# Cross attention in a decoder layer: one load of queries for the row maxima of two heads, on keys whose masked places are filled

## The chip, the cores and the metric

One core of a Trainium2 chip runs the whole kernel in one launch. The metric is the device time in microseconds, from a median of runs. Its engines work side by side, each on its own queue in program order: TensorE (PE: products, and PEld: the loads of its stationary operand), VectorE (DVE), ScalarE (ACT), GpSimd (POOL) and SyncE (SP), which here only issues DMAs. Products land in PSUM, which this kernel uses as eight banks of 128 x 512 fp32.

## The reference

Four sequences of 1024 rows and 256 features pass a decoder layer: windowed causal self-attention, cross attention on 77 context rows, and a quantised feed-forward part. The change touches the middle one alone (16 heads of 16 features):

```python
x = x + attn(layernorm(x), w_qkv, w_out)                      # windows of 128, causal
x = x + xattn(layernorm(x), ctx, ctx, mask, Wq, bq, Wk, bk, Wv, bv, Wo, bo)
x = x + ffn(layernorm(x), ...)                                # int8-like rounding

def xattn(Q, K, V, mask, Wq, bq, Wk, bk, Wv, bv, Wo, bo):
    q = heads(Q @ Wq.T + bq)          # [4, 16, 1024, 16]
    k = heads(K @ Wk.T + bk)          # [4, 16, 77, 16]
    v = heads(V @ Wv.T + bv)
    scores = einsum('bhqd,bhkd->bhqk', q, k) / 4
    scores = where(mask == 0, -inf, scores)
    attn = softmax(scores)            # needs the row maximum first
    return merge(einsum('bhqk,bhkd->bhqd', attn, v)) @ Wo.T + bo
```

In the inputs all rows of the mask are alike (the same keys are masked for every query).

## The kernel before

**Heads and groups.** The 16 heads stand in two groups g of eight. In a group, partitions are cut into four strips j of 32; a strip holds two heads, `o` = 0 and 1, of 16 features each. A projected tile `q[g, o]` (128 partitions x 1024 queries) keeps the rows of head o in each strip; the other head's 16 rows are zero and partly used as extra rows: one will hold minus the row maximum, one is constant 1. For keys `kx` the matching rows hold 1 and the mask bias (0 or -1e30). So one product of depth 32 gives score + mask - maximum, and ACT only takes the exponential.

**Two products of the same scores.** For each (g, o) the scores are formed twice. `maxima` forms them with queries on partitions (bank `sc_n`, line 742 for cross attention: stationary a tile of 128 queries, moving 77 keys); DVE reduces them to the row maxima (line 768). `put_maxima` turns the maxima on TensorE (line 779), copies them to SBUF on ACT (`mxT`, line 783) and writes them with four DMAs on SP's queue (line 786) into a row of each strip of `q[g, o]`. Then `weights` forms the scores with keys on partitions (bank `sc_t`, line 841: stationary 77 keys, moving 512 queries), ACT takes exp (line 844), and `weighted_values` multiplies with the values (line 866).

**Units and slots.** The work is a list of units (job, g, o, u). Jobs are S0 S1 S2 X0 S3 X1 X2 X3 (S self-attention, X cross attention, the digit is the sequence); an S job has 16 units, an X job 8 (u = two halves of 512 queries). A loop over slots issues, in this order: `early` work, values of an older unit (`ps_av`, line 856 or 866, with DVE's lines 880 to 902), tasks (projections `ps_p`, out-projections `ps_op`, turns `ps_t`, preparation), DVE work beside, `puts`, then `maxima` of the unit five slots ahead (LEAD = 5), then `weights` of the slot's own unit. Each engine takes what is issued in that order. PSUM banks go round all these uses, so a product can wait for ACT or DVE to have read a bank.

**Projections.** `project` forms 512 queries of all heads of a group (16 instructions of line 304), and ACT writes two masked copies, one for each o (line 363 for cross attention: bias and scale both from per-partition columns).

**When maxima are put.** For (g, o) whose first unit has slot tau, with m units per (g, o), `put_maxima` is in slot tau + m - LEAD: tau - 1 for S jobs (m = 4), tau - 3 for X jobs (m = 2).

**Preparation of cross attention** is a list of pieces, three slots apart from slot 5 on, one step a slot: biases; Wk; the context (loaded by one DMA, turned by eight products of line 490, copied by DVE, line 495); keys (line 502, written by four DVE instructions of line 510); Wv; values of the context; the mask row; Wq; Wo. All of it falls into jobs S0 and S1. A branch on whether the mask's rows are alike picks one of two whole programs; with these inputs the first, `alike`, runs.

## Time and profile before

| | us |
|---|---|
| median of 3 runs (lowest, highest) | 669.54 (668.43, 670.75) |
| the profiled execution: its time | 669.67 |
| its span, first to last instruction | 668.0 |
| mean granted TensorE clock | 0.981 |
| line 742 (maxima of X), 1024 instructions from 270.8 to 524.1: product busy, load busy | 36.5, 31.7 |
| line 768 (DVE maxima of X), 128 x 468 ns | 51.9 |
| line 363 (ACT, projected queries of X), 32 x 774 ns | 23.1 |
| line 779 (turn of maxima), 32 instructions | 9.1 |
| line 786 (DMAs of maxima), 128 of 4 KB, issue of one on SP's queue | 0.63 |
| keys and context, lines 490, 502 (PE), 495, 510 (DVE), once | 0.8, 2.3, 0.9, 2.1 |

An fp32 product is two instructions in the trace (two loads, two products), so the 16 products of a unit of line 742 stand as 32. Durations of products are modelled and overlap; what a group of them takes is read from the start of the first to the start of what follows. By stages: X0's maxima run from 270 to 307 us beside S2 and X0's own weights, X1's from 399 to 435, X2's and X3's to 524; the feed-forward part starts near 560.

### The profile page before, as it was taken

Reading aid. Unit: us, or ns where it says so; the run is one execution under the profiler, and the core shown is the slowest. Engines: PE = TensorE matmul, PEld = TensorE weight load, DVE = VectorE, ACT = ScalarE, POOL = GpSimd, SP = SyncE. Lnnn points to the kernel's source line nnn. Section 1 sums busy time; section 2 is a strip of 40 time slices with the busy share of each in tenths; the row PEclk is TensorE's granted clock in tenths of the full one; section 3 lists DMA queues with packets and bytes.
Section 4 is the critical chain, followed back from the end, with each engine's and each line's share of the span. In section 5 each row is a group of like instructions: output and inputs, shape, how many; then the busy total and the mean of one; then the engine's idle time right before and its main releaser. Section 6 shows DMA issues by size and latency. Waiting matters only on the chain.

```text
span 668.0 us, 20224 instructions
## 1 busy us (share of the span) xinstructions
PE 619.9 (93%) x7862; PEld 355.8 (53%) x7862; DVE 542.9 (81%) x1922; ACT 367.8 (55%) x672; POOL 268.9 (40%) x520
## 2 busy tenths in 40 slices
PE   9989999999999998999999999999999997888774
PEld 6466556566555565654446666554443445333564
DVE  6588887878769799768997996897978787799896
ACT  2535454653555644655565356447556465688392
POOL 3135632455324567660035777616611141111032
PEclk9979799999999999999999999999999999899898
DMA  8100100000000000000000000000000020000057
GB/s 290 46 2 17 38 2 3 20 5 4 19 26 11 11 2 19 5 19 12 9 11 11 11 24 26 5 3 4 3 3 4 4 95 17 1 0 1 1 96 163
DMA packets 18081, 17.43 MB, mean 26 GB/s; under 512 B 2999, under 2 KB 17336, under 8 KB 17976
## 3 DMA queue, kind: packets, MB, share of 16 engines
q1 hardware_dynamic: 15239, 13.69, 6.4%
q0 software_dynamic: 1904, 1.84, 2.1%
q8 instruction: 64, 1.05, 0.7%
q10 hardware_dynamic: 832, 0.53, 0.3%
q14 instruction: 42, 0.34, 0.2%
HBM read 9.47 MB, written 6.03 MB: 23 GB/s over the span
## 4 chain that ended last, share of the span: by engine, by line
PE 62%; DVE 25%; ACT 6%; issue 5%; POOL 1%; DMA 0%; DVEq 0%; ACTq 0%
PE ps_p L304 13%; PE ps_av L856 8%; PE sc_t L812 8%; PE sc_n L727 7%; PE ps_op L304 6%; PE ps_av L866 4%; PE sc_t L841 3%; PE ps_v L304 3%; PE sc_n L742 3%; DVE junk L757 3%; DVE bnst L192 2%; DVE o_sb L880 2%; PE ps_idle L117 2%; PE pg L1393 2%; DVE aT L902 2%
## 5 line engine op out<-in xcount | busy, mean ns | idle before, releaser
L757 DVE CUSTOM_DVE_ANT_0 junk<-sc_n,cboth 128x256 bf16<-128x256 f32 (+1 forms) x512 | 172.5, 402 | 34.5 <-PE sc_n L727 34.4
L822 ACT ACTIVATE pt<-sc_t 128x512 f32<-128x512 f32 (+1 forms) x256 | 125.4, 576 | 92.6 <-PE sc_t L812 92.6
L826 POOL TENSOR_SCALAR_AFFINE_SELECT pt<-pt 128x256 f32<-128x256 f32 x256 | 102.0, 407 | 114.8 <-ACT pt L822 104.6
L812 PE MATMUL sc_t<-shared 32*128 32x256 f32 (+1 forms) x1024 | 91.1, 382 | 2.4 <-DVE mx L757 0.6
L844 ACT ACTIVATE ptx<-sc_t 77x512 f32<-77x512 f32 x128 | 65.3, 597 | 36.9 <-PE sc_t L841 36.9
L727 PE MATMUL sc_n<-shared 32*128 32x256 f32 (+1 forms) x1024 | 79.1, 398 | 1.3 <-ACT shared L369 0.7
L812 PEld LDWEIGHTS sc_t<-shared 32*128 32x128 f32 x1024 | 68.0, 188 | 15.6 <-ACT shared L363 2.5
L320 POOL TENSOR_SCALAR xn<-x,mv,rs 128x256 f32<-128x256 f32 x56 | 70.0, 1256 | 0.0
L160 POOL TENSOR_SCALAR ve<-mv 128x4 f32<-128x4 f32 x20 | 4.6, 232 | 156.4 <-DVE mv L194 156.3
L880 DVE STREAM_TRANSPOSE o_sb<-ps_av 128x512 f32<-128x512 f32 x63 | 45.0, 714 | 26.0 <-PE ps_av L856 15.9
L727 PEld LDWEIGHTS sc_n<-shared 32*128 32x128 f32 x1024 | 49.8, 190 | 30.2 <-DVE mx L757 11.1
L856 PE MATMUL ps_av<-pt,vt 128*32 128x256 f32 (+1 forms) x1152 | 60.1, 352 | 3.0 <-DVE mx L757 2.6
L304 PE MATMUL ps_p<-shared,w_s 128*32 128x512 f32 x512 | 60.5, 595 | 2.4 <-DVE mx L768 1.3
L768 DVE TENSOR_REDUCE mx<-sc_n 128x4 f32<-128x308 f32 x128 | 51.9, 468 | 8.5 <-PE sc_n L742 8.3
L856 PEld LDWEIGHTS ps_av<-pt,vt 128*32 128x32 f32 x1152 | 35.2, 111 | 31.7 <-DVE mx L757 6.4
L841 PE MATMUL sc_t<-shared,kx 32*77 32x512 f32 x256 | 45.9, 599 | 0.0
L757 DVE DVE_READ_ACCUMULATOR2_ANT mx<- 128x1 f32 x512 | 42.5, 83 | 0.1
L866 PE MATMUL ps_av<-ptx,vx 77*32 77x512 f32 x256 | 36.0, 605 | 3.4 <-DVE mx L768 2.5
L363 ACT ACTIVATE shared<-ps_p,bq_p,qrows 128x512 f32<-128x512 f32 x32 | 23.1, 774 | 26.0 <-PE ps_p L304 26.0
L742 PEld LDWEIGHTS sc_n<-kx,shared 32*128 32x128 f32 x1024 | 31.7, 186 | 10.1 <-DVE mv L194 1.7
L742 PE MATMUL sc_n<-kx,shared 32*128 32x77 f32 x1024 | 36.5, 277 | 0.0
L1408 ACT ACTIVATE act<-pg,gsc 128x512 f32<-128x512 f32 x44 | 29.2, 688 | 11.6 <-PE pg L1393 9.0
(201 smaller groups left out, 986.7 us busy)
## 6 DMA issues: line engine op xcount, KB each, us to landing
x<-in_x_dram SPq DMA_DIRECT2D x8, 512.0 KB
shared<-mxT SPq DMA_DIRECT2D x128, 4.0 KB
out_dram<-x SPq DMA_DIRECT2D x7, 256.0 KB
out_dram<-shared POOLq DMA_DIRECT2D x7, 256.0 KB, 4.5
out_dram<-shared SPq DMA_DIRECT2D x7, 256.0 KB
w_s<-in_L_attn_w_qkv_dram SPq DMA_DIRECT2D x2, 384.0 KB
raw_d<-in_L_ffn_w_down_dram SPq DMA_DIRECT2D x2, 352.0 KB
raw_f<-in_L_ffn_w_gate_dram SPq DMA_DIRECT2D x5, 128.0 KB
```

Source lines behind the costliest of these rows:

```text
L304: nc.tensor.matmul(out[r], lhsT[:, r], rhs, skip_group_check=True, **on)
L320: eng.tensor_scalar(xn, xb[job.b][:, t, :], job.st[hf].mv[:, i, 0:1], job.st[hf].rs[:, i : i + 1], ALU.subtract, ALU.mult,)
L727: nc.tensor.matmul(banks[j][:, (i + 1) * 2 * P - n : (i + 1) * 2 * P], q[r, t * P : (t + 1) * P], k[r, k0 * P : k0 * P + n], start=True, s ...
L742: nc.tensor.matmul(banks[j][:, i * SK : (i + 1) * SK], q[r, t * P : (t + 1) * P], k[r, :], start=alike, stop=alike or i == HT - 1,)
L757: nc.vector.tensor_tensor_reduce(out=junk[:, 2 * P - n :], in0=banks[j][:, (i + 1) * 2 * P - n : (i + 1) * 2 * P], in1=cboth[:, 2 * P - n ...
L812: nc.tensor.matmul(banks[j][:, w : w + n], k[r, t * P : (t + 1) * P], q[r, t * P : t * P + n], start=True, stop=True,)
L822: nc.scalar.activation(pt.rearrange("p i a q -> p (i a q)")[:, :w], banks[j][:, :w], AF.Exp)
L826: nc.gpsimd.affine_select(out=pt[:, :, 0, :], in_=pt[:, :, 0, :], compare_op=ALU.is_ge, fill=0.0, base=0, pattern=[[0, 2], [1, P]], channe ...
L841: nc.tensor.matmul(banks[j][:SK], k[r, :], q[r, s], start=alike, stop=True)
L844: nc.scalar.activation(pt, banks[j][:SK], AF.Exp)
L856: nc.tensor.matmul(ps[j * SL : (j + 1) * SL, (a0 - t0) * P : (a1 - t0) * P], slot_of(job.vs[kb // 2][:, kb % 2], heads[j]), job.pts[g, o, ...
L866: nc.tensor.matmul(ps[j * SL : (j + 1) * SL, :], slot_of(vx[:, job.b], heads[j]), job.pts[g, o, j, hf], start=True, stop=True,)
```

## The change

Only the program for alike rows is changed, and in it cross attention alone.

1. **Preparation.** Before the context is loaded, a new piece `for_maxima` is put into the list, with four steps: `load_keymask` (the context, now by two DMAs, and one mask row on 77 partitions), `pick` (a 77 x 77 matrix that takes every unmasked key to itself and every masked key to the first unmasked one: seven DVE instructions and one POOL select), `context(True)` (the context times that matrix), and `keys_for_maxima` (keys from it without mask rows, written to a new tile `kmx` in which both heads' keys of a strip stand side by side, zero in the other head's rows). The plain context is loaded and turned again three slots later; all later pieces come three slots later.
2. **Projection.** For o = 0 ACT writes both heads' queries unmasked (scale an immediate, bias `bq_s`); o = 1 as before.
3. **Maxima.** One product of a tile of 128 queries with 154 columns of `kmx` gives the scores of both heads. A unit now takes two query tiles of both heads in place of four tiles of one: 8 products of 154 columns in place of 16 of 77, and DVE reduces the same 308 columns a bank.
4. **Masking later.** `part_heads` rewrites `q[g, 0]` in place on ACT (128 x 1024) to what it was before: head 0's rows and the constant row.
5. **Put.** One `put_maxima` a group in place of two: one turn and one copy of 64 rows, then eight DMAs. It and `part_heads` are in slot tau + 2m - LEAD = tau - 1 of o = 0.

```diff
@@ project
-                if job.kind == "X":
+                if job.kind == "X" and job.both and o == 0:
+                    nc.scalar.activation(
+                        dst, ps, AF.Identity, bias=job.bqs[:, g : g + 1], scale=QSCALE
+                    )
+                elif job.kind == "X":
@@ prep_cross: biases
+                    nc.vector.tensor_scalar(bq_s, raws["q"], QSCALE, None, ALU.mult)
...
+                            if alike and name == "k":
+                                nc.vector.tensor_copy(raws["bk"][:, :, o], dst[:, :, o])
@@ prep_cross: context
                 def load_context():
-                    raws["c"] = stage.tile([SK, B, D], F32, name="craw", tag="stage")
-                    nc.sync.dma_start(out=raws["c"], in_=ctx_in.rearrange("b k d -> k b d"))
+                    for h in range(2):
+                        raws["c", h] = stage.tile([SK, B // 2, D], F32, name="craw", tag="stage")
+                        nc.sync.dma_start(
...
-                def context():
+                def context(chosen=None):
...
+                            if chosen is None:
+                                nc.tensor.transpose(
+                                    ps[:, b * SK : (b + 1) * SK], raw, ident[:SK, :SK]
+                                )
+                            else:
+                                nc.tensor.matmul(
+                                    ps[:, b * SK : (b + 1) * SK],
+                                    raw,
+                                    raws["pick"],
+                                    start=True,
+                                    stop=True,
+                                )
...
+                def load_keymask():
+                    load_context()
+                    raws["v"] = small.tile([SK, SK], I32, name="vrow", bufs=1)
+                    nc.sync.dma_start(out=raws["v"], in_=mask[0, :].partition_broadcast(SK))
+                def pick():
+                    nc.vector.tensor_scalar(valid, raws["v"], 0.0, None, ALU.not_equal)
+                    nc.gpsimd.affine_select(
+                        out=below,
...
+                    nc.vector.tensor_reduce(held_by[:, 0:1], below, AX.X, ALU.max)
+                    nc.vector.tensor_tensor(sel, valid, ident[:SK, :SK], ALU.mult)
+                    nc.vector.tensor_reduce(held_by[:, 1:2], sel, AX.X, ALU.max)
+                    nc.vector.tensor_tensor(
+                        first, held_by[:, 1:2], held_by[:, 0:1], ALU.is_gt
+                    )
+                    nc.vector.tensor_scalar(valid, valid, -1.0, 1.0, ALU.mult, ALU.add)
+                    nc.vector.scalar_tensor_tensor(sel, valid, first, sel, ALU.mult, ALU.add)
+                def keys_for_maxima():
+                    for g in range(NP):
...
+                        for o in range(NS):
+                            nc.vector.tensor_scalar(
+                                kmx[:, g, :, o * SK : (o + 1) * SK],
+                                ps[:, : B * SK].rearrange("p (b k) -> p b k", k=SK),
+                                rows[o],
+                                raws["bk"][:, g, o : o + 1],
...
+                for_maxima = [load_keymask, pick, lambda: context(True), keys_for_maxima]
                 return [
                     [load_biases, biases],
                     transposed(Wk, "wk_x"),
+                    *([for_maxima] if alike else []),
                     [load_context, context],
@@ maxima
+                if job.kind == "X" and alike:
+                    pair = NH * o + u
+                    w = NS * SK
+                    for i in range(2):
+                        t = 2 * pair + i
+                        for j in range(NJ):
+                            r = slice(j * SL, (j + 1) * SL)
+                            nc.tensor.matmul(
+                                job.nb[j][:, i * w : (i + 1) * w],
+                                job.q[g, 0][r, t * P : (t + 1) * P],
+                                kmx[r, g, job.b, :],
+                                start=True,
+                                stop=True,
+                            )
+                    for j in range(NJ):
+                        nc.vector.tensor_reduce(
+                            job.mx[g][:, :, j, 2 * pair : 2 * pair + 2].rearrange("p o i -> p i o"),
+                            job.nb[j][:, : 2 * w].rearrange("p (i o k) -> p i o k", i=2, o=NS),
...
@@ put_maxima
+            def part_heads(job, g, o):
+                q = job.q[g, 0]
+                nc.scalar.activation(q, q, AF.Identity, bias=nextrow[o], scale=rows[o])
...
+                nc.tensor.transpose(ps[:n, :P], mx, ident)
+                nc.scalar.copy(mxT[:n], ps[:n, :P])
+                for k in range(n // NT):
+                    o_, j = divmod(k, NJ) if two else (o, k)
+                    row = j * SL + (1 - o_) * HD
                     nc.sync.dma_start(
-                        out=job.q[g, o][row : row + 1, :],
-                        in_=mxT[j * NT : (j + 1) * NT, :],
+                        out=job.q[g, o_][row : row + 1, :],
+                        in_=mxT[k * NT : (k + 1) * NT, :],
                     )
@@ the list of slots
-                        puts.setdefault(tau + m - LEAD, []).append((job, g, o))
+                        if S_ or not alike:
+                            puts.setdefault(tau + m - LEAD, []).append((job, g, o))
+                        elif o == 0:
+                            at = tau + NS * m - LEAD
+                            early.setdefault(at, []).append((part_heads, (job, g, o)))
+                            puts.setdefault(at, []).append((job, g, o))
```

## The prediction

> **What bounds the kernel now.** I read the busy shares first, then the chain of waits over cross attention, then the timeline of single slots there, because a share over the span hides which wait ends last.
>
> ```profile
> PE 619.9 (93%) x7862; PEld 355.8 (53%) x7862; DVE 542.9 (81%) x1922; ACT 367.8 (55%) x672; POOL 268.9 (40%) x520
> ```
>
> TensorE looks full. In the chain of waits (start, length, what) a typical slot of X2 reads so:
>
> ```profile
> 456.06 1.00 PE ps_av L866 x8
> 457.05 1.72 PE ps_p L304 x16
> 458.77 1.06 PE sc_n L742 x32
> 459.83 1.69 PE sc_t L841 x8
> 461.52 1.04 PE ps_av L866 x8
> ```
>
> All five are TensorE's, the maxima of line 742 among them; but line 841 took 1.69 there. A slot in which it waits for nothing, and then one like that above (timeline; start, length, engine, line):
>
> ```profile
> 509.18 1.04 PE L841 MATMUL sc_t<-shared,kx 32*77 32x512 f32 x8
> 510.14 1.06 PE L866 MATMUL ps_av<-ptx,vx 77*32 77x512 f32 x8
> ...
> 468.66 1.13 PE L742 MATMUL sc_n<-kx,shared 32*128 32x77 f32 x32
> 468.80 1.45 ACT L363 ACTIVATE shared<-ps_p,bq_p,qrows 128x512 f32<-128x512 f32 x2 [1.10 <-PE ps_p L304]
> 469.61 1.76 PE L841 MATMUL sc_t<-shared,kx 32*77 32x512 f32 x8
> 470.30 0.21 PEld L841 LDWEIGHTS sc_t<-shared,kx 32*77 32x77 f32 x2 [0.53 <-ACT shared L363]
> 471.31 1.07 PE L866 MATMUL ps_av<-ptx,vx 77*32 77x512 f32 x8
> ```
>
> Free, line 841 needs 0.96 us to the next product. In the second slot it needs 1.70: its last bank is the projection's, and ACT's two copies of line 363 release that at 470.25. They start at 468.80, when the projection has ended, whatever line 742 does meanwhile. So there the slot's length is projection, then 1.45 of ACT, then two products of 0.49 on one strip; line 742 lies beside ACT.
>
> I sorted all 32 units of line 742 by what ends the line 812 or 841 behind them. 14 wait for ACT's projection copies as here (at 270.8, 274.9, 285.0, 294.4, 398.9, 403.1, 409.6, 442.1, 453.4, 458.7, 468.7, 487.5, 498.9, 504.3). Two wait for ACT's copy of line 341 (306.6, 413.3). 14 lie in stretches where the chain runs through DVE (lines 880 to 902, 192, then 768) and TensorE waits at its end. Two are free: 300.7 and 508.2, and behind the second DVE follows with 0.12 us of slack.
>
> **The change: the maxima.** A unit of line 742 takes 0.95 us from 403.07 to 404.02, 29.7 ns an instruction. The price of 154 columns is not in the trace; the nearest rows are self-attention's:
>
> ```profile
> 311.61 0.94 PE L727 MATMUL sc_n<-shared 32*128 32x128 f32 x16
> 312.37 1.04 PE L841 MATMUL sc_t<-shared,kx 32*77 32x512 f32 x8
> ...
> 317.77 1.15 PE L727 MATMUL sc_n<-shared 32*128 32x256 f32 x16
> 318.74 1.62 PE L841 MATMUL sc_t<-shared,kx 32*77 32x512 f32 x8
> ```
>
> 16 of 256 columns take 0.97 us (60.6 ns each); 8 of 128 and 8 of 256 take 0.76, so 128 columns cost 34.4. By interpolation 154 cost 39.7, the unit 16 x 39.7 = 0.63, a saving of 0.32; at the price of 256 columns it is nothing. Over 32 units that is 10.1 us of TensorE, but on the path only where TensorE ends last: the two free units (0.32 and 0.12), almost nothing elsewhere: 0.5 us. DVE's reductions are the same 128 of 468 ns.
>
> The Trainium skill (Perfetto Trace Analysis, "Identifying the Most-Contended Engine") holds matmul busy time for no measure of how full TensorE is, and load busy time for a better one: 93% against 53% here. By the 93% this part would save some 9 us; by the rule TensorE has room and it saves next to nothing, which the waits above bear out.
>
> **Fewer turns.** 8 of the 16 X instructions of line 779 go, 0.21 us each (453.21 to 453.42). Four stand in stretches of DVE and cost nothing there. At 409.4, 453.2 and 498.7 ACT's copy after line 363 is what goes (about 0.13 us later than the projection's own release), at 300.5 the whole 0.21: 0.6 us, of which I count 0.4. DVE is late next.
>
> **Cheaper projection copies.** For o = 0 the scale becomes an immediate.
>
> ```profile
> L363 ACT ACTIVATE shared<-ps_p,bq_p,qrows 128x512 f32<-128x512 f32 x32 | 23.1, 774 | 26.0 <-PE ps_p L304 26.0
> L367 ACT ACTIVATE shared<-ps_p,qrows 128x512 f32<-128x512 f32 x32 | 20.3, 684 | 19.4 <-PE ps_p L304 19.4
> ```
>
> Two column operands cost 774 ns, one 684; so 0.09 less in each of the 13 of those 14 slots whose copies are line 363 (at 294.4 they are S3's): 1.2 us, on the path. Lower bound nothing.
>
> **Part_heads and the later put.** The same ACT copy at 1024 columns: lines 822 at 384 and 512 columns (496 and 602 ns) give 0.83 ns a column, so 0.774 + 0.42 = 1.2 us, eight times, from SBUF. It queues on ACT before the slot's projection copies, `mxT` and exponentials. In seven of the eight slots ACT is idle long enough or only `mxT` and line 341 move (X2's first by 0.4, hidden behind DVE). At X3's first (508.4) `mxT` is 1.1 late, and if its bank is needed by line 841 at once, the path loses up to 0.6.
>
> The put of o = 0 moves from slot tau - 3 to tau - 1, past the queues of TensorE, ACT and SP. A DMA of line 786 holds SP's queue 0.72 us, the fourth row's packets end 3.5 us after the first issue, and the only wait that the trace shows (line 812 at 59.39 for the third row, issued from 54.75) puts the semaphore about a microsecond behind the data. So the turn must stand some 5 us ahead of the weights. It does at six of eight places: 6.2 us at X0's and X2's first, 7 at X0's and X1's second, 6.5 at X2's second, 5.7 at X1's first (a wait of 0 to 0.3). At X3 it doesn't: 4.1 us (508.01 to 512.09) and 2.2 (529.93 to 532.17), late by about 1.7 each. Behind them queue line 841's last strips, then `ps_av`; but there DVE has its own work until 516.5 and 537.9, and ACT takes line 941 first. The other four DMAs (o = 1) are wanted two slots later. Together I take 0.5, bounds 0 and 4.3 (two of 1.7, 0.6, 0.3).
>
> **Preparation,** in S1's neighbourhood near 95 to 130 us, where it stood once:
>
> ```profile
> 98.00 0.75 PE L490 MATMUL ps_c<-ident,craw 77*128 77x77 f32 x8
> 98.68 1.92 PE L304 MATMUL ps_p<-shared,w_s 128*32 128x512 f32 x16
> ...
> 108.82 2.34 PE L502 MATMUL ps_kx<-cT,wk_x 128*128 128x308 f32 x8
> 111.09 1.15 PE L727 MATMUL sc_n<-shared 32*128 32x256 f32 x16
> 112.06 0.60 PE L812 MATMUL sc_t<-shared 32*128 32x256 f32 x6
> 112.92 1.13 PE L812 MATMUL sc_t<-shared 32*128 32x256 f32 x10 [0.25 <-DVE kx L510]
> ```
>
> Slot by slot in the new order: slot 12 loses the 0.68 us of line 490 (on the chain) and gains `pick`, eight small instructions; its POOL select queues behind the four selects of slot 11 (to 100.07), its DVE part ends near 101.4 where DVE idles 1.93 up to 101.70: 0.2. Slot 13 gains the chosen context as true products, 16 instructions for the 8 of 85 ns (0.68 / 8): 1.4 (bounds 0.7, and 4.5 at the 284 ns of line 502). Slot 14 keeps a set of keys. Slot 15 gains the turn: DVE is its chain (115.84 to 119.49), so two copies of 0.43 count: 0.9. Slot 17 gains the other keys: 2.27 us between projection and line 727 (125.64 and 127.47 before), of which 0.8 lies beside ACT's copies, for which line 812 waited there (1.78 us, about 1.0 where it is free); with DVE's four of 0.59, which line 812 awaits as at 112.92, the slot grows by 1.5 to 2.4: 2.0. `biases` gets three DVE instructions of 0.25 near 60: 0.2. Loads have a slot's lead or more; Wv, Wq, Wo only shift. Sum 4.0, bounds 1.7 (DVE's copies and `pick` hidden, cheap products) and 7.1 (the dear products).
>
> **Sum.** -0.5 - 0.4 - 1.2 + 0.5 + 4.0 = +2.4 on the span of 668.0: 670.4. The execution profiled had 669.67, 0.13 over the median of the runs, 669.54; so I predict 669.54 + 2.4 = 671.9, for this case alone 670.5 to 674.
>
> **Rivals.** *TensorE was the bound after all:* 18 units stand as TensorE's in the chain of waits; 18 x 0.32 + 0.85 (four whole turns) + 1.2 - 0.5 = 7.3 saved, 4.0 paid: 666.2. For it the chain's names; against it the stretched line 841. *The preparation hides:* DVE's idle 1.93, 0.69 and 1.29 us between 98 and 108 take its share, and it costs 1.7: 669.6. Against it ACT's wait at 102.1 and DVE's chain at 115.8. *The late put decides* (slower): at X3's two places, from the point where the rows land after ACT and DVE have run dry, 4.3 in place of 0.5: 675.7. Against it, DVE's own chain from 511.3 to 520.
>
> **Chances.** The forecast 0.45, TensorE 0.21, hidden preparation 0.22, late put 0.12. Within 0.3% (2.0 us) is about what a measurement can't tell from no change. Faster: 0.20 from the second, 0.03 from the third; same: 0.05, 0.01, 0.17; slower: 0.40, 0.02, 0.12. Range 665.5 to 676.0: from rival to rival, and a little below the lowest for line 742's own price.
>
> **What would show it.** 512 instructions of 154 columns near 40 ns from start to start; line 841's successors still ending at ACT's copies, with the old length less 0.1; the time from 95 to 130 longer by some 4; X1 to X3 shorter by 1 to 3; waits for the DMA of line 786's successor at X3 alone. A region from 395 to 530 shorter by over 5, or S1 grown by under 2, makes it wrong; so does a DMA wait at most of the eight places.

## The result and the profile after

| | before | after |
|---|---|---|
| runs beside each other: median of 7 each (lowest, highest) | 669.92 (668.43, 671.81) | 675.42 (674.37, 684.39) |
| ratio, with its 95% interval | | 1.0113 (1.0073 to 1.0153) |
| profiled execution: time, span | 669.67, 668.0 | 674.55, 672.8 |
| mean granted TensorE clock of the profiled execution | 0.981 | 0.983 |

The change made the kernel slower by 5.5 us in the median, and it spread the runs: 3.4 us from lowest to highest before, 10 after.  The forecast was 671.9, range 665.5 to 676.0.

The page's busy times hardly show it (busy us, share of the span, instructions):

```profile
PE 623.6 (93%) x7361; PEld 349.9 (52%) x7366; DVE 548.0 (81%) x1938; ACT 373.7 (56%) x672; POOL 269.3 (40%) x521
```

The trace has 501 fewer products on TensorE, and its busy time grew by 3.7 us. The groups by shape (busy us, mean ns of one) confirm the prices of the single instructions:

```profile
L805 PE MATMUL sc_n<-kmx,shared 32*128 32x154 f32 x512 | 26.0, 315 | 0.0
...
L367 ACT ACTIVATE shared<-ps_p,bq_p,qrows 128x512 f32<-128x512 f32 x16 | 12.3, 771 | 0.0
L363 ACT ACTIVATE shared<-ps_p,bq_s 128x512 f32<-128x512 f32 x16 | 11.0, 687 | 25.3 <-PE ps_p L304 25.2
L882 ACT ACTIVATE shared<-shared,nextrow,rows 128x1024 f32<-128x1024 f32 x8 | 10.0, 1251 | 0.0
```

The copy with an immediate takes 687 ns in place of 774; the pass of line 882 takes 1.25 us where 1.2 was estimated. What the shorter maxima are worth is seen in the slot that stood in the prediction at 468.66 (timeline after; start, length, engine, line):

```profile
471.52 0.81 PE L805 MATMUL sc_n<-kmx,shared 32*128 32x154 f32 x16
471.66 0.69 ACT L363 ACTIVATE shared<-ps_p,bq_s 128x512 f32<-128x512 f32 x1 [1.43 <-PE ps_p L304]
...
472.15 2.00 PE L951 MATMUL sc_t<-shared,kx 32*77 32x512 f32 x8
472.24 0.77 ACT L367 ACTIVATE shared<-ps_p,bq_p,qrows 128x512 f32<-128x512 f32 x1
473.06 0.21 PEld L951 LDWEIGHTS sc_t<-shared,kx 32*77 32x77 f32 x2 [0.76 <-ACT shared L367]
...
473.69 1.63 DVE L813 TENSOR_REDUCE mx<-sc_n 128x4 f32<-128x308 f32 x4
474.21 0.16 PEld L976 LDWEIGHTS ps_av<-ptx,vx 77*32 77x32 f32 x8 [0.94 <-DVE mx L813]
474.22 1.06 PE L976 MATMUL ps_av<-ptx,vx 77*32 77x512 f32 x8
```

The maxima take 0.63 us (471.52 to 472.15) where they took 0.95, as interpolated; and line 951 behind them takes 2.07 (to 474.22) where it took 1.70. Its last bank is released by ACT at the end of line 367, whatever TensorE saved. ACT's two copies end 1.49 us after the maxima's start (473.01), before 1.59 (470.25 from 468.66): 0.1 less, as predicted; the 0.32 of the maxima is not seen. From the maxima's start to the next `ps_av` it is 2.70, before 2.65. That is because the slot now ends at another engine: `ps_av` waits for DVE's first reduction of line 813, which starts at 473.69, later than ACT's release. So this slot shows that the maxima were not on the path, but not that ACT's 0.1 was gained in it.

The preparation, TensorE's lines after, beside the last units of S0 and the first of S1:

```profile
103.25 2.01 PE L511 MATMUL ps_c<-pick,craw 77*128 77x77 f32 x16
105.19 1.93 PE L304 MATMUL ps_v<-w_s,shared 128*32 128x256 f32 x32
...
109.06 2.34 PE L556 MATMUL ps_kx<-cT,wk_x 128*128 128x308 f32 x8
...
115.92 0.75 PE L507 MATMUL ps_c<-ident,craw 77*128 77x77 f32 x8
...
128.42 2.34 PE L577 MATMUL ps_kx<-cT,wk_x 128*128 128x308 f32 x8
```

The chosen context takes 1.94 us; a second turn (line 507) and a second set of keys (line 577) follow. And this is the place in X3 of which the prediction said "late by about 1.7", TensorE's timeline after (in square brackets: idle time before):

```profile
532.60 0.30 PE L890 MATMUL ps_mx<-ident,mx 128*64 128x128 f32 x1
532.83 1.10 PE L951 MATMUL sc_t<-shared,kx 32*77 32x512 f32 x8
533.86 1.06 PE L976 MATMUL ps_av<-ptx,vx 77*32 77x512 f32 x8
535.11 3.87 PE L951 MATMUL sc_t<-shared,kx 32*77 32x512 f32 x8 [0.19 <-ACT ptx L954]
538.91 1.94 PE L976 MATMUL ps_av<-ptx,vx 77*32 77x512 f32 x8
540.78 2.01 PE L951 MATMUL sc_t<-shared,kx 32*77 32x512 f32 x8
542.71 1.87 PE L976 MATMUL ps_av<-ptx,vx 77*32 77x512 f32 x8
544.51 1.10 PE L951 MATMUL sc_t<-shared,kx 32*77 32x512 f32 x8
```

The unit at 535.11 is long because its four strips come one by one: single instructions of line 951 start at 535.11, 535.84, 536.56 and 537.28, each 1.9 us after its row's DMA was issued (the first at 533.22, the next ones 0.72 us later each). From 538.91 everything takes twice its time, `ps_av` 1.87 to 1.94 where it took 1.06. The busy times by windows say why (length, busy and number of instructions of PE, PEld, DVE, ACT, POOL, then the granted clock):

```profile
534.20:537.60 3.40, 3.21 (x15) 0.83 (x8) 2.15 (x5) 3.40 (x9) 0.62 (x1) 0.99 0.03 6
537.60:541.00 3.40, 3.40 (x15) 0.42 (x16) 3.04 (x13) 2.01 (x4) 0.49 (x2) 0.50 0.41 143
541.00:544.40 3.40, 3.40 (x16) 0.33 (x12) 1.65 (x3) 1.54 (x4) 2.16 (x6) 0.50 0.93 326
```

The granted clock is 0.50 from 537.6 to 544.4. In the profile of before it is 1.00 there. The page's busy time of TensorE (3.21 of 3.40) hides the hole: only 15 products were under way between 534.2 and 537.6, and 11 of them started there.

**A ledger of the two traces.** For each unit of weights I took the start of its first product in each profiled execution, subtracted that of a second profile of the kernel before (668.42 us, span 666.7), and set the difference at S0's twelfth unit (95 us) to nought. What lies ahead of that differs by up to 1.7 us either way between the executions of the table, in part by where half-clock windows fall between 42 and 76 us. The columns are the starts of seven units in that second profile: S0's fourteenth in the midst of the new preparation (107), S1's second behind its dear steps (127), S2's ninth ahead of all cross attention (254), the last unit of X2 (508), X3's fifth and sixth (531, 533; the fifth is the one with the late rows, so that its lateness shows at the sixth) and the last unit of X3 (540).

| us later than before | 107 | 127 | 254 | 508 | 531 | 533 | 540 |
|---|---|---|---|---|---|---|---|
| before, first profile | 0.0 | 0.0 | 0.0 | -0.2 | -0.2 | -0.2 | -0.2 |
| after | 1.4 | 4.4 | 5.1 | 3.0 | 3.9 | 7.4 | 6.8 |
| after, second profile | 1.7 | 4.7 | 5.4 | 3.3 | 4.2 | 7.9 | 9.1 |
| prep_only | 1.4 | 4.5 | 5.7 | 5.5 | 5.5 | 5.5 | 5.8 |
| cheap_dve | 0.0 | 3.6 | 3.4 | 1.6 | 2.5 | 4.5 | 5.8 |
| split_load | 0.0 | 0.0 | 0.0 | -0.2 | -0.2 | -0.2 | -0.2 |
| late_put | 0.0 | 0.0 | 0.0 | -0.2 | 0.0 | 1.9 | -0.1 |
| one_dma_before | 0.0 | 0.0 | -0.3 | -0.6 | -0.6 | -0.6 | -0.7 |
| rows_one_dma | 1.4 | 4.4 | 3.9 | 1.4 | 2.4 | 2.2 | 1.9 |
| column_scale | 1.4 | 4.4 | 3.9 | 2.6 | 4.0 | 3.9 | 3.6 |
| part_twice | 1.4 | 4.4 | 3.9 | 5.6 | 7.1 | 6.9 | 6.7 |
| sooner | 1.6 | 4.6 | 5.3 | 8.4 | 11.8 | 11.8 | 12.1 |
| cheap_one_dma | -0.1 | -0.1 | -0.5 | -2.9 | -1.9 | -2.1 | -2.4 |

So the change reads: preparation +5.1, cross attention up to 508 us -2.1, X3's first units +0.9, the late rows +3.4 (their last strip already at half clock) and what the clock takes behind them.

### The profile page after: what moved, and what is told of

The parts are those of the page before. It is cut to its first block, busy times and chain, and to the rows that moved or that the text cites. A ratio compares the mean times of both kernels' runs of the same rounds, so it can differ in the third digit from the quotient of the medians.

```text
span 672.8 us, 19197 instructions
## 1 busy us (share of the span) xinstructions
PE 623.6 (93%) x7361; PEld 349.9 (52%) x7366; DVE 548.0 (81%) x1938; ACT 373.7 (56%) x672; POOL 269.3 (40%) x521
## 4 chain that ended last, share of the span: by engine, by line
PE 66%; DVE 23%; ACT 5%; issue 4%; POOL 1%; DMA 0%; DVEq 0%; ACTq 0%; POOLq 0%; SPq 0%
PE ps_p L304 12%; PE sc_t L922 8%; PE sc_n L830 8%; PE ps_av L966 8%; PE ps_op L304 5%; PE ps_av L976 5%; PE sc_t L951 5%; PE ps_v L304 3%; DVE junk L860 3%; DVE o_sb L990 2%; PE ps_idle L117 2%; DVE bnst L192 2%; PE pg L1508 2%; PE sc_n L805 2%; DVE hq L1611 1%
## 5 line engine op out<-in xcount | busy, mean ns | idle before, releaser
L922 PE MATMUL sc_t<-shared 32*128 32x256 f32 (+1 forms) x1024 | 93.4, 379 | 3.1 <-ACT shared L367 0.6
L922 PEld LDWEIGHTS sc_t<-shared 32*128 32x128 f32 x1024 | 69.7, 187 | 17.7 <-ACT shared L367 4.5
L966 PE MATMUL ps_av<-pt,vt 128*32 128x256 f32 (+1 forms) x1152 | 58.6, 346 | 3.7 <-DVE mx L860 3.5
L951 PE MATMUL sc_t<-shared,kx 32*77 32x512 f32 x256 | 55.8, 617 | 0.5 <-DVE x L1030 0.3
L192 DVE BATCH_NORM_STATS2 bnst<-x 128x6 f32<-128x256 f32 x88 | 32.3, 411 | 1.8 <-DMA x<-in_x_dram 1.6
L1508 PE MATMUL pg<-xqT,wgT 128*128 128x512 bf16 x77 | 24.4, 392 | 10.0 <-ACT xqT L1490 7.2
L373 ACT ACTIVATE shared<-ps_p,onerow,rows 128x512 f32<-128x512 f32 x32 | 23.2, 776 | 18.0 <-PE ps_p L304 18.0
```

The lines of the kernel that those rows point to most:

```text
L922: nc.tensor.matmul(banks[j][:, w : w + n], k[r, t * P : (t + 1) * P], q[r, t * P : t * P + n], start=True, stop=True,)
L951: nc.tensor.matmul(banks[j][:SK], k[r, :], q[r, s], start=alike, stop=True)
L966: nc.tensor.matmul(ps[j * SL : (j + 1) * SL, (a0 - t0) * P : (a1 - t0) * P], slot_of(job.vs[kb // 2][:, kb % 2], heads[j]), job.pts[g, o, ...
```

## The experiments

All times are medians, ratios are against runs of the kernel before on the same chip, beside them.

### Parts of the change alone: prep_only, cheap_dve, after_again, before_again

`prep_only` is the changed kernel with maxima, put and projection as before:

```diff
@@ max_bias, maxima
-                if job.kind == "X" and alike:
+                if False:
@@ put_maxima
-                two = job.kind == "X" and alike
+                two = False
@@ puts
-                        if S_ or not alike:
+                        if True:
@@ project
-                if job.kind == "X" and job.both and o == 0:
+                if False:
```

> The kernel before with only the new preparation (the first valid key picked, the chosen context, the second set of keys, three more bias instructions, the context in two loads); maxima, turns, put and projection copies stay those of before, and the new keys are read by nobody. Theory: the preparation is what makes the change slower. Then this is 4 to 6 us above the kernel before (5.2 by the two traces, where S1's start to S2's shifted), and all of it arises between 95 and 150 us of the profile. Rival: the loss comes from cross attention, the late put and ACT's extra pass; then this is within 2 us of the kernel before.

Measured: 674.65 us (674.47 to 675.61) against 669.40, ratio 1.0083 (1.0070 to 1.0097). The preparation costs 5.3 us, and the ledger puts 5.7 of it between 95 and 254 us. The theory had all of it by 150 us; at 152 it stands at 2.6, and the moved pieces bring the rest (5.2 at 196). But these runs lie within 1.2 us of each other: the spread of the changed kernel is not from here.

`cheap_dve` leaves `for_maxima` out and writes `kmx` from the same products as `kx`:

```diff
-                    *([for_maxima] if alike else []),
@@ keys: after the write of kx
+                            if alike:
+                                nc.vector.tensor_scalar(
+                                kmx[:, g, :, o * SK : (o + 1) * SK],
+                                ps[:, : B * SK].rearrange("p (b k) -> p b k", k=SK),
+                                rows[o],
+                                raws["bk"][:, g, o : o + 1],
+                                ALU.mult,
+                                ALU.add,
+                            )
```

> The changed kernel without pick, chosen context and second set of key products: the keys for the maxima are written by four more DVE instructions from the same products as kx, so the maxima run over the masked keys too (the replacement by the first valid key is left out). Theory: cross attention as changed is worth 1 to 2 us and the preparation costs 5; with the four DVE instructions (2.1 us busy, on DVE's chain in S1) in its place this is 0 to +1.5 us against the kernel before, and 4 us under the changed one. Rival (late put and ACT's pass decide): 3 us or more above the kernel before.

Measured: 675.01 us (672.39 to 677.64), ratio 1.0079 (1.0051 to 1.0106). The theory missed, and the number is the rival's, 5.6 above the kernel before. But the rival is right only in part, because what stands in place of the dear preparation is dear as well. In the profile TensorE waits for these DVE instructions twice behind the keys, 0.26 and 1.33 us, the clock is halved from 116.1 to 119.5, and the ledger has 3.6 lost by 127 us. The other loss is in X3, 4.2 from 508 to 540 us, with a half-clock window of 17.1 us from 539.4 on. The runs differ by more than 5 us. The mean granted clock of its runs was 0.970 to 0.985, that of the kernel before 0.984 to 0.991; the three runs at 0.980 and over took 672.4 to 673.2, the three at 0.975 and under 676.8 to 677.6.

> The changed kernel once more, unaltered, for the price of the whole change with more rounds and for a second profile of it. Theory: 4.5 to 6.5 us above the kernel before. The first profile granted half the TensorE clock at 537.6 to 544.4 us. If that belongs to the program it stands there again; if it belongs to the execution it moves or goes, and the tail from X3's last units to 560 us is some 3 us shorter.

Measured: 677.17 us (673.23 to 681.05), ratio 1.0109 (1.0076 to 1.0142). In the second profile the clock falls at the same place, 537.3 us, but stays down for 20.5 us in place of 6.8. In these two profiles the place is the program's and the length the execution's. Not every execution need have it: over both sets of runs the changed kernel has four with a mean clock of 0.987 or more, and they took 673.2 to 675.2. Behind the fall every group takes about twice its time (TensorE's timeline, second profile of the changed kernel):

```profile
535.26 4.13 PE L951 MATMUL sc_t<-shared,kx 32*77 32x512 f32 x8 [0.19 <-ACT ptx L954]
539.33 1.94 PE L976 MATMUL ps_av<-ptx,vx 77*32 77x512 f32 x8
541.19 2.00 PE L951 MATMUL sc_t<-shared,kx 32*77 32x512 f32 x8
...
550.73 4.09 PE L976 MATMUL ps_av<-ptx,vx 77*32 77x512 f32 x16
```

> The kernel before, unaltered, for a second profile of it. The first granted half the clock at 42 to 49, 69 to 76, 575 to 578, 629 to 633 and from 663 us. If the windows belong to the program, they stand there again; if to the execution, the one at 69 to 76 moves or goes.

Measured: 668.42 us, one run. No half-clock window at 69 us this time and none near 537: of the windows of before, the one at 69 us belongs to the execution.

### The late put and the clock: late_put, rows_one_dma, fill_wait

`late_put` brings one thing of the change into the kernel before:

```diff
-                        puts.setdefault(tau + m - LEAD, []).append((job, g, o))
+                        wait = 2 if alike and job is jobs[-1] and (g, o) == (NP - 1, 0) else 0
+                        puts.setdefault(tau + m - LEAD + wait, []).append((job, g, o))
```

> The kernel before with one thing of the change alone: the put of X3's second group, first head, two slots later, just ahead of the second head's put, so that its four rows are as late as in the changed kernel. Theory: a half-clock window appears near 534 to 545 where the kernel before has none, the runs spread over 5 us or more, and the median is 3 to 8 us above the kernel before: 672 to 678. Rival (a wait of 1.7, hidden behind VectorE as the prediction had it): 669 to 671.

Measured: 670.91 us (667.63 to 678.23), 12 runs, ratio 1.0035 (1.0008 to 1.0061). The median is under the theory's and within the rival's, the spread is the theory's. The runs fall in two kinds: five with a mean clock of 0.977 or under took 673.3 to 678.2, seven with 0.981 or over 667.6 to 671.3; of 40 runs of the kernel before beside these and the first four, none was under 0.982. The profiled execution is one of the second kind, with the clock whole and the rows as late as designed (TensorE's timeline of `late_put`):

```profile
530.31 1.07 PE L866 MATMUL ps_av<-ptx,vx 77*32 77x512 f32 x8
531.44 3.22 PE L841 MATMUL sc_t<-shared,kx 32*77 32x512 f32 x8
534.59 1.07 PE L866 MATMUL ps_av<-ptx,vx 77*32 77x512 f32 x8
```

Line 841 takes 3.15 to the next product, the ledger has 1.9 at 533 us, and at 540 us it is gone (-0.1). So the prediction's reading, that a wait of 1.7 hides behind VectorE there, holds where the clock stays up; where it falls, the same wait costs 4 to 9 us (673.3 to 678.2 against some 669). Of the five runs only the mean clock is known, not the place where it fell.

`rows_one_dma` leaves the turn as late as it is and lets the rows land together:

```diff
-                for k in range(n // NT):
-                    o_, j = divmod(k, NJ) if two else (o, k)
-                    row = j * SL + (1 - o_) * HD
-                    nc.sync.dma_start(
-                        out=job.q[g, o_][row : row + 1, :],
-                        in_=mxT[k * NT : (k + 1) * NT, :],
-                    )
+                for o_ in range(NS) if two else (o,):
+                    k = NJ * (o_ if two else 0)
+                    row = (1 - o_) * HD
+                    nc.sync.dma_start(
+                        out=job.q[g, o_][row:P:SL, :],
+                        in_=mxT[k * NT : (k + NJ) * NT, :],
+                    )
```

> The changed kernel with one DMA for the four rows of a head in place of four, so that the rows of a late put land together, some 2 us sooner for the last strip. Theory (the late put at X3's second place starves TensorE between 535.1 and 537.3, and the granted clock falls to half for 6.8 to 20.5 us behind it): the four strips of X3's unit no longer come 0.72 us apart, the half-clock window near 537 is gone, the spread of the runs shrinks to about 2 us and the time is what the preparation costs (5.2) less what cross attention gains (1.7): 671.5 to 674. Rival (the clock falls for another reason, or at random): window and spread stay, 674 to 679.

Measured: 671.15 us (670.30 to 672.07), 12 runs, ratio 1.0026 (1.0011 to 1.0040): a little better than expected, and the spread is gone. The unit again (TensorE's timeline of `rows_one_dma`):

```profile
530.59 1.10 PE L951 MATMUL sc_t<-shared,kx 32*77 32x512 f32 x8
531.62 1.07 PE L976 MATMUL ps_av<-ptx,vx 77*32 77x512 f32 x8
532.96 1.10 PE L951 MATMUL sc_t<-shared,kx 32*77 32x512 f32 x8 [0.27 <-DMA shared<-mxT]
533.98 1.06 PE L976 MATMUL ps_av<-ptx,vx 77*32 77x512 f32 x8
```

One wait of 0.27 for the DMA in place of strips that came 0.72 apart, and no half-clock window between 71 and 565 us. The single DMA, four times as large, landed about as soon as one of the four: it was issued at 530.98, and the strips started 1.98 us later.

`fill_wait` asks whether TensorE's holes are what the clock follows:

```diff
+                        if alike and job is jobs[-1] and (g, o, u) == (NP - 1, 0, 0):
+                            idle(banks[j], 8)
                         nc.tensor.matmul(banks[j][:SK], k[r, :], q[r, s], start=alike, stop=True)
```

> The changed kernel, rows as late as there, but eight dummy products of zeros ahead of each strip of X3's late unit, into the bank that the strip is about to overwrite, where TensorE waits for the rows anyway. It tells the wait from the clock. Theory: the wait by itself costs at most 1.7, the clock behind it 3 to 9; with TensorE kept busy no half-clock window stands near 537, no run is above 676, the median is 672.5 to 675. Rival (the wait itself is the loss): as the changed kernel, 675 to 678, windows or not.

Measured: 678.00 us (676.53 to 679.14), 6 runs, ratio 1.0129. The time is the rival's, but not for its reason (TensorE's timeline of `fill_wait`):

```profile
535.69 1.05 PE L117 MATMUL sc_t<-zeros 128*128 128x256 bf16 x8
536.67 1.08 PE L953 MATMUL sc_t<-shared,kx 32*77 32x512 f32 x2
537.68 1.05 PE L117 MATMUL sc_t<-zeros 128*128 128x256 bf16 x8
...
543.64 1.06 PE L978 MATMUL ps_av<-ptx,vx 77*32 77x512 f32 x8
```

The dummy products take the whole array, so the strips can no longer run beside one another: the unit takes 7.95 us (535.69 to 543.64) where a free one takes 1.03. The fillers were mis-sized: 0.98 us each, and strips that run alone behind them. About the clock it agrees with the theory, though the unit's own time changed too: no half-clock window from 50 to 582 us, no run under a mean clock of 0.984, and a spread of 2.6 us.

### The other terms: one_dma_before, split_load, column_scale, part_twice

`one_dma_before` is the same edit of the put in the kernel before (one `dma_start` for the four rows).

> The kernel before with one DMA for the four rows of a head in place of four, in self and cross attention, nothing else. It is the control for the two runs with one DMA. Theory: in the kernel before the rows are in time (one wait for them in the trace), so it is worth little: 0 to -1.0, 668.4 to 669.6. Then the 3.5 us between the run with the preparation alone and the changed kernel with one DMA are cross attention's gain. Rival (the rows' queue costs the kernel before something too, in self attention): 666 to 668, and the gain of cross attention is only what is left of the 3.5.

Measured: 668.66 us (666.48 to 669.70), ratio 0.9980 (0.9969 to 0.9992): 1.3 us faster, within the theory's 668.4 to 669.6, though the difference is more than its 1.0; in the ledger 0.3 comes before 254 us and 0.3 in X0 to X2. So of the 5.7 parts in a thousand between `prep_only` (1.0083) and `rows_one_dma` (1.0026), 2.0 are the DMA's and 3.7, or 2.5 us, remain for cross attention.

`split_load` is `prep_only` without the piece `for_maxima`.

> The kernel before with the smallest part of the new preparation: the context in two loads and the three small bias instructions, without pick, chosen context and second keys. Theory: 0.2 us (0 to 0.7), so 669.4 to 670.2, and the 5.2 us of the preparation lie in pick, chosen context, the second turn and the second keys. Rival: the loads hold up SP's queue in S1 and cost 1 us or more.

Measured: 669.35 us (668.43 to 671.77), ratio 1.0001 (0.9988 to 1.0014). The loads and the bias instructions cost nothing that can be measured.

`column_scale` is `rows_one_dma` with the cheap copy's column given back:

```diff
-                        dst, ps, AF.Identity, bias=job.bqs[:, g : g + 1], scale=QSCALE
+                        dst, ps, AF.Identity, bias=job.bqs[:, g : g + 1], scale=job.qcol
```

> The changed kernel with one DMA a head, with the scale of the first head's projection copy taken from a column again instead of an immediate (same value). It prices the term 'cheaper projection copies'. As predicted (13 copies of 0.09 on the path): 1.2 us above the changed kernel with one DMA, 672.3. Rival (ACT's copies are hidden, the gain comes from the maxima's shorter products): 0 to 0.3 above it, 671.2 to 671.5.

Measured: 673.24 us (671.29 to 676.90), ratio 1.0047 (1.0030 to 1.0065) beside 1.0026 for `rows_one_dma`: 2.1 parts in a thousand, 1.4 us, with intervals that overlap. The ledger is sharper: from 254 to 508 us `rows_one_dma` gains 2.4 and `column_scale` 1.3, a difference of 1.2. That is the predicted term. (In its profile the clock fell at 516.2 us, for 3.4; the further 0.5 behind 508 us comes with that.) One DMA a head does not keep the clock up everywhere: these runs spread by 5.6 us again, two of them with a mean clock of 0.977.

`part_twice` is `rows_one_dma` with the pass of `part_heads` repeated; the second changes nothing.

> The changed kernel with one DMA a head, and ACT's pass that clears the other head's rows done twice in a row (the second changes nothing). It prices part_heads: 8 more passes of 1.25 us, 10 us of ACT. If the pass is hidden at most places, as predicted: 0 to 1.5 us above the changed kernel with one DMA, 671.2 to 672.7. If it is on the path at most places: 4 to 10 us above it.

Measured: 676.47 us (675.08 to 677.84), ratio 1.0101 (1.0085 to 1.0118), 5 us over `rows_one_dma`: the second outcome, half of the added 10 us. Against `rows_one_dma`, unit by unit, the ledger's 4.7 comes in steps at the pass's own places: 1.9 us at X0's first unit, 0.7 at its fifth, 0.3 at X1's first, 1.3 over X2's first three, 0.6 at X3's first. The first pass shows no such step at X0's first unit, where the changed kernel moves by -0.3 as the first profile of before does. So one pass fits into ACT's slack and two do not. But most of the largest step is the clock's: TensorE waits 1.18 us for ACT's `mxT`, which by itself makes 0.3, the clock is halved from 295.0 to 298.4, and the projection there takes 3.45 us in place of 1.85. Doubling overstates the pass's price, and the run says how little slack is left.

### Putting it together: cheap_one_dma, sooner, sooner_one_dma, cheap_sooner

`cheap_one_dma` has no `for_maxima`, POOL writes `kmx` from `kx` (four times `kmx = kx * rows[o]`), and the rows go by one DMA.

> The changed kernel without pick, chosen context and second key products, the keys for the maxima made by POOL from kx (four instructions; masked keys are not replaced, so the maxima run over them too), and the rows of a head by one DMA. Both suspected costs are gone, what is left is cross attention's gain (1.7) against the split load and POOL's four instructions in S1: 667 to 669.5, a little under the kernel before. If cross attention's gain was never there, 669.5 to 671.

Measured: 667.54 us (666.22 to 669.00), 12 runs, ratio 0.9970 (0.9955 to 0.9984): faster than both kernels. The ledger shows no cost of POOL's keys at all (-0.1 at 127 us) and the gain of 2.4 from 254 to 508 us. It leaves out the replacement of masked keys in the maxima, which matters where a masked key's score is far above all others (not run); `one_dma_before`, which leaves nothing out, beats both kernels too.

`sooner` moves pass and put behind the weights of the slot before:

```diff
-                            early.setdefault(at, []).append((part_heads, (job, g, o)))
-                            puts.setdefault(at, []).append((job, g, o))
+                            late.setdefault(at - 1, []).append((part_heads, (job, g, o)))
+                            late.setdefault(at - 1, []).append((put_maxima, (job, g, o)))
```

> The changed kernel with part_heads and the put one step earlier in the order: behind the weights of the slot before instead of behind the weighted values, projections and output projections of its own slot; still four DMAs a head. At X3's second group that is 4.5 us earlier (1.07 of ps_av and 3.64 of ps_op stood ahead of the turn). Theory (the lateness in the order starves TensorE): no half-clock window near 537, the strips of X3's unit come together, a spread of some 2 us, 671 to 673.5. Rival (the turn now stands on TensorE ahead of work that was free and waits there for VectorE's last reductions, 0.5 to 0.9 us at each of eight places): 674 to 678, without the window.

Measured: 683.34 us (679.62 to 684.96), ratio 1.0205 (1.0182 to 1.0228). Worse than the rival. At X3 the strips do come together (TensorE's timeline of `sooner`):

```profile
534.60 0.30 PE L890 MATMUL ps_mx<-ident,mx 128*64 128x128 f32 x1 [1.32 <-DVE mx L813]
534.83 1.38 PE L976 MATMUL ps_av<-ptx,vx 77*32 77x512 f32 x8
535.97 5.07 PE L304 MATMUL ps_op<-wo_x,aT 128*32 128x256 f32 x64
540.97 1.10 PE L951 MATMUL sc_t<-shared,kx 32*77 32x512 f32 x8
542.00 1.07 PE L976 MATMUL ps_av<-ptx,vx 77*32 77x512 f32 x8
```

Line 951 takes 1.03 at 540.97, so the order alone cures the lateness, with four DMAs too (the slow `ps_op` ahead of it gave the rows 1.4 us more). But the turn now waits for VectorE's reductions in front of everything else on TensorE. By the table of waits of `sooner` (us in total, times, longest):

```profile
PE ps_mx L890 <- DVE mx L813: 5.7, 6, 1.3
```

That is 5.7 us in six waits, and in the ledger 3.1 are lost from 254 to 508 us where the changed kernel gains 2.1. Behind the wait that ends at 534.6 stands a half-clock window of its own, 535.5 to 538.9, in which `ps_op` takes 5.07 in place of 3.64.

> The same earlier put, with one DMA a head. Against the earlier run of one DMA alone (671.15, 1.0026 of the kernel before): if the 0.9 us lost between X3's first and fifth unit come from the late turn, this is 0.5 to 1 us below it (670 to 670.7); if they come from ACT's pass, which is as long as ever, 0 to +0.5; if the turn's wait for VectorE costs at all eight places, 2 to 4 above it.

> The run with cheap keys (POOL's four instructions, masked keys not replaced in the maxima) and one DMA a head, with the earlier put. 667.54 or 0.9970 of the kernel before without it; with it 666.5 to 667.5 if the earlier turn helps at X3, 668 to 671 if it waits for VectorE at all eight places.

Measured: 680.88 us, ratio 1.0166 (1.0148 to 1.0184), and 679.06 us, ratio 1.0122 (1.0096 to 1.0147): both took the dear branch, and worse. From 254 to 508 us they lose 6.0 and 4.5, with half-clock windows on the way (296.9 and 447.1; 440.5). Whether the 0.9 us between X3's first and fifth unit come from the turn or from the pass is therefore not answered by them.

## Why the prediction was right and wrong

**What bounds the kernel: right.** The 10 us of TensorE that the shorter products free were not on the path. Of the rival "TensorE was the bound after all" (7.3 saved) little is left: with copies as dear as before (`column_scale`), maxima, turns, put and pass together gain 1.3 from 254 to 508 us, part of it by the one DMA (0.35). In the slot quoted above line 951's last strip waits for ACT's release, as named beforehand, and 0.32 saved ahead of it moved nothing; what ends that slot is by now DVE.

**Maxima, turns and copies: right, in size too.** Predicted -0.5, -0.4 and -1.2; the ledger has -2.1 for the changed kernel from 254 to 508 us, and -1.2 for the copies by themselves. Maxima and turns were not run apart from each other.

**The preparation: right in kind, too small.** Predicted 4.0, bounds 1.7 to 7.1; measured 5.1 in the trace of after, 5.3 by `prep_only`. Slot 15 (+0.9) and 17 (+2.2 against 2.0) hit. The chosen context was mis-sized: slot 13 grew by 2.1, where its products were put at 1.4; they take 1.94, or 121 ns each, and not the 85 ns of the turns (115.92 to 116.60), by which 16 would be 1.4. And "Wv, Wq, Wo only shift" was priced at nothing: from 127 to 254 us the moved pieces cost 0.7 in the changed kernel and 1.3 in `prep_only`, and with one DMA a head they gain 0.5. Where a moved piece meets other work decides its price, also when none of its instructions changed. "The preparation hides", the second rival, is refuted: only the loads, the bias instructions and `pick` were free (slot 12 lost 0.7, as much as line 490 took there).

**The late put: the step that failed.** The prediction found the place (X3's second group), the lateness (1.7) and the cover (VectorE's own work until 537.9), and charged 0.5 for it and the pass together. `late_put` bears place, lateness and cover out in its profiled execution: 1.9 late at 533 us, nothing left at 540. So does X3's first group in the trace of after: its last two strips also come late (the unit takes 2.39 us from 514.51), and the ledger goes from 3.4 to 3.2 over it. What failed is the overlap: the prediction took it that behind a wait which DVE's own work hides, TensorE goes on at its old pace. In both profiles of the changed kernel TensorE works on one strip at a time for 2.2 us, half the clock is granted from 537.6 or 537.3 us on, for 6.8 us in one and 20.5 in the other, and TensorE becomes the bound of the stretch that was VectorE's. In the trace of after that and the late strips make +2.9 between 531 and 540 us, in the second profile +5.0. The third rival, "the late put decides", gave 675.7 and so came near in time, with the wrong mechanism: it summed waits at two places, of which the late rows at the first cost nothing, and did not have the clock. That is luck.

**The pass of part_heads: right, barely.** One pass hides, as argued; `part_twice` shows that a second one would have cost 5, of which its profile puts 1.6 on the clock.

**The sum with the measured terms,** trace of after: 5.1 - 2.1 + 0.9 + 2.9 = 6.8 at 540 us, against a predicted +2.4: 1.1 of the miss is preparation, 0.4 X3's first units, 2.9 the late strips with the clock. (The spans differ by 6.1, 672.8 against 666.7, the medians by 5.5.) The term predicted at 0.5 for pass and put measures 3.8 in all, within its bounds of 0 to 4.3; I took the value near the lower end because VectorE covered it.

**Left open:** what the 0.9 us at X3's first to fifth unit are, which every kernel with the new maxima loses, with cheap keys and one DMA too (0.4 of them at the first unit, where the second pass cost another 0.6); what the late rows cost the changed kernel where its clock stays up, since both of its profiles have the fall; and beforehand, in which executions the clock falls: with `late_put` the mean clock was low in five of twelve (the last section has an estimate of what it hangs on).

## What to carry to other kernels

A wait that is hidden behind another engine is only free while it leaves the clock alone: where TensorE would run dry in the cover, price the stretch behind it at half clock too, and look at the mean clock of every run, not only at the median. Rows that are wanted together should land together: one DMA over four strips instead of four was worth more here (1.3 us in the kernel before, some 6 in the medians of the changed one) than all the time that the shorter maxima gained. And a saving on an engine that is full by busy time but not on the path buys little, while the preparation that it needs is paid in full.

## What the runs showed of the hardware

- The granted clock took two values in the profiles, 1.0 and 0.5, its low one in stretches of 3.4 us or multiples of it (6.8, 17.1, 20.5), and in each of the 17 profiles all changes lie on one grid of 3.413 us, to within 0.01. The Trainium skill (TensorE: Matmul & The Clock Gate, "Part 1: The HAM clock gate (the "warmup" mystery)") describes such a gate, with a free-running window of 3413 ns, whose clock falls after an idle window; the lengths agree, and a window that runs freely fits that the same wait makes the clock fall in some runs only. But here no window was idle: 15 products were under way in the one ahead of the fall at 537.6 us, those of line 951 on one strip of four at a time, and TensorE never stood still for 3.4 us. The same page ("Why this matters for your kernels") asks for no gaps over some 3 us between bursts; here that was too generous, since between 76 and 562 us no wait of TensorE ahead of a fall was longer than 1.5 us, and the measurement decides.
- How little work went with a fall can be estimated from the traces. For each window of the grid, add up the columns of TensorE's products, each weighted with the share of the 128 x 128 array that it occupies (rows and columns rounded up to 32) and spread over its recorded duration. Between 48 and 562 us the 17 profiles have 20 windows behind which the full clock fell, with 861 to 1480 such columns (1193 and 1358 in the two profiles of the changed kernel). The other 2487 windows at full clock have 3171 in the median; seven of them lie under 1480, none under 1354. In the profile of `late_put` the grid cuts the stretch of single strips at 532.8 us into windows of 1774 and 1707, and the clock stays up; so it does behind X3's first late rows in the trace of after, in a window of 1669. So whether the same wait costs the clock seems to hang on where the grid happens to lie. This is an estimate, with modelled durations, made after the fact; what the chip counts, no run here shows.
- Products on one strip of 32 rows run beside those of the other strips, but in `fill_wait` not beside products on all 128: eight dummy products ahead of each strip turned a unit of 1.03 us into one of 7.95.
- One DMA of 16 KB over four partitions 32 apart let its strips start 1.98 us after its issue; each of four of 4 KB took 1.9 us, but, issued 0.72 us apart, they made the last strip 2.2 us later than the first.
